# A GRU over 128 steps on one core: zero products during the loads, weight sums moved into the first step, x turned one step at a time, biases spread in two parts

## The chip, the cores and the metric

The kernel runs on one core of a Trainium2 chip. A core has TensorE (PE, with PEld for the loading of its stationary operand), VectorE (DVE), ScalarE (ACT), GpSimd (POOL) and SyncE (SP), which here only issues DMAs. The metric is the device time of one execution in microseconds; the median of several executions is compared.

## The reference

x is 64 sequences of 128 steps with 512 numbers each, `cond_1024` the first hidden state (64 x 512). The output is x plus the hidden states of a GRU:

```
for t in range(T):
    comb = concatenate([x_t, h])
    z = sigmoid(comb @ Wz + bz)
    r = sigmoid(comb @ Wr + br)
    h_cand = tanh(concatenate([x_t, r * h]) @ Wh + bh)
    h_new = (1 - z) * h + z * h_cand
    y_t = h_new
    h = tanh(h_new @ Wp + bp) if (t + 1) % 4 == 0 and t < T - 1 else h_new
return x + y
```

Wz, Wr and Wh are 1024 x 512: the upper 512 rows meet x (the kernel's `wx`), the lower 512 meet h or r*h (`wh`). Everything is float32.

## The kernel before

**Layout.** A state of 64 x 512 lies as 128 partitions x 256: partition s*64 + b holds half s of row b. A product with a 512 x 512 matrix is four units k in the order `ORDER`; each unit (`product`, through `products`, L177) is two matmuls, one for each half of the columns, written to the two halves of the partitions. A float32 matmul is two matmul records, so a unit is four records of 64 x 256. The stationary operand is the state turned round, 128 x 64. `turn` (L202) does the turning: eight bf16 transposes on PE into the two PSUM banks `turn_ps[0]` and `turn_ps[1]`, and one copy for each bank (L193) into `xT`, `hT` or `rhT`, on DVE or ACT as the caller says. The activations of a step use another part of the same two banks (`act_ps`).

**A step t** runs through these places in program order:

1. R: `product(slots[R], hT, wh[R], k)` for four k, onto a slot of PSUM that already holds the share of x and the bias
2. for t below 5, turns of x (`turn_x`, two of them), with their copies on ACT
3. `read_out`: pending read-outs of x products
4. sigmoid of R on ACT, `rh` = r*h on DVE (L599)
5. Z: four units; then the turn of rh, its copies on DVE; sigmoid of Z and of -Z on ACT, `keep` = (1-z)*h on DVE (L615)
6. `fill(places[0])`: units of x products for later steps, from `queue`
7. H: four units with `rhT`; `read_out`; tanh on ACT, two DVE operations for each half (L638, L643) that make h
8. `fill` again, the turn of h, between its halves a unit of `fill`; with every fourth step the extra product with `wp`
9. in steps 0 and 1, two more turns of x; then POOL's additions

Each engine takes its instructions in this program order; the schedule is by hand.

**Shares of x.** Step 0 gets its share directly (`first`), steps 1 to 7 by `plain(t)`, twelve units each, with a read-out of two DVE additions (L409, L414). In steps 0, 1 and 2 the queue holds `plain(2t+2)` and `plain(2t+3)`, and the places are 12, 9, 1 and 2 units. From step 8 on, four steps at a time are worked out together by `batches`, a two-level scheme of seven products in place of eight, which needs sums of blocks of `wx` and sums of the turned x:

- `sum_outer` (L300 to L302): six DVE subtractions and additions of 128 x 768 that fill `tw[2]`, `tw[3]`, `tw[4]` from `wx`; after it, `sum_inner` (L309 to L311) and for some blocks `sum_inner_1` (L314) on POOL: blocks 1, 2 and 3 from `wx`, blocks 6, 7 and 4 from `tw`.
- `sum_raw12`, `sum_s12` (L323 to L326, L341, L342), `sum_s34`: sums of turned x on POOL for one group of four steps. The first group of the batches is `FIRST` = 2, steps 8 to 11. x of steps 8 to 15 is read from two tiles `early`, whose buffers later hold batch results.
- The batches start in step 3, in the places of `fill`; step 3 also has three `sum_inner_1` on DVE before `rh`.

**The start.** SP issues x of steps 0 and 1 and half of each gate's `wx`, then `wh`, more of x, and `wp`; ACT issues the biases, the other halves of `wx` and the first state. The bias rows are spread over 64 partitions by matmuls with a row of ones (L160): four records of 512 columns into `rc` (R and H), four into `zp` (Z and p), then four DVE copies to `bias` and one POOL subtraction to `bias_d`. Then x of steps 0 and 1 is turned with copies on DVE, then come `first` and `plain(1)` unit by unit, with the turn of the first state after the R units. Before the step loop stand `read_out()`, `sum_outer()` on DVE and the eighteen plus three POOL operations of `sum_inner` and `sum_inner_1`.

Of the kernel before, what the change touches and what calls it, by code (L numbers as in the profile page):

```python
# [10 lines left out]
BF16 = mybir.dt.bfloat16  # L11
# [6 lines left out]
def kernel(  # L18
# [29 lines left out]
    nc = tc.nc  # L48
    B, T, D = x.shape
    H = h0.shape[1]  # L50
    P = 128
    S = 2
    N = H // S
# [4 lines left out]
    FIRST = 2  # L58
    R, Z, H_ = range(3)
# [4 lines left out]
    one = ctx.enter_context(tc.tile_pool(name="one", bufs=1))  # L64
# [74 lines left out]
    rc = ps_c.tile([P, 2, N], F32, name="rc")  # L139
    zp = ps_c.tile([P, 2, N], F32, name="zp")  # L140
    slots = (rc[:, 0, :], zp[:, 0, :], rc[:, 1, :])
    slot_p = zp[:, 1, :]
    scratch = [ps_c.tile([P, 2 * N], F32, name=f"scratch_{n}") for n in "qrax"]
# [9 lines left out]
    bias = const.tile([P, C, 4, P], F32, name="bias")  # L153

    def cut(ps):
        return ps.rearrange("p (c n) -> p c n", c=C)

    for a, ps in enumerate((rc, zp)):
        for s in range(S):
            nc.tensor.matmul(  # L160
                ps[s * B : (s + 1) * B, :, :],
                lhsT=ones,
                rhs=bias_row[:, 2 * a : 2 * a + 2, ts(s, N)],
                start=True,
                stop=True,
            )
    for i, ps in ((R, slots[R]), (H_, slots[H_]), (Z, slots[Z]), (3, slot_p)):
        nc.vector.tensor_copy(bias[:, :, i, :], cut(ps))
    bias0 = bias[:, 0, 0:3, :]
    bias_d = const.tile([P, 3, P], F32, name="bias_d")  # L170
    nc.gpsimd.tensor_sub(bias_d, bias[:, 1, 0:3, :], bias0)


    def products(ps, lhs, rhs, start=False):
# [11 lines left out]
    def product(ps, lT, w, k, start=False):  # L186
        s0, c0 = divmod(k, C)
        products(ps, lT[:, c0, ts(s0, B)], lambda s: w[:, k, ts(s, N)], start)
# [6 lines left out]
    def turn(src, dst, c, name, eng):  # L195


        pt = turn_ps[c][:, :P].bitcast(BF16).rearrange("p (w n) -> p w n", w=2)
        for s in range(S):
            words = src[:, c * P + s * B : c * P + (s + 1) * B].bitcast(BF16)  # L200
            for w in range(2):
                nc.tensor.transpose(  # L202
                    pt[s * B : (s + 1) * B, w, :],
                    words.rearrange("p (n w) -> p w n", w=2)[:, w, :],
                    ident16,
                )
        copy(
            eng,
            dst[:, c, :].bitcast(U16).rearrange("p (n w) -> p n w", w=2),
            pt.bitcast(U16).rearrange("p w n -> p n w"),  # L210
        )

    def new_T(tag, name):
        return two.tile([P, C, P], F32, tag=tag, name=name)
# [7 lines left out]
    def new_xT(g):  # L222
        if g not in xT:
            xT[g] = xtp.tile([P, Q4, C, P], F32, tag="xT", name=f"xT_{g}")

    def turn_x(t, eng=nc.scalar):
        g, i = divmod(t, Q4)
        new_xT(g)
        src = xr[g] if g < 2 else early[g]
        for c in range(C):  # L230
            turn(src[:, i, :], xT[g][:, i], c, f"xT_{t}", eng)
# [36 lines left out]
    def outer(kb, nb, ka):  # L268

        return wx[:, ka * C + kb, :, :].rearrange("p g (s n u) -> p n s g u", s=S, n=C)[:, nb]  # L270
# [12 lines left out]
    def inner(i, ka, na):  # L283
        return OPERAND[i](ka)[:, :, :, ts(na, P // 2)]
# [13 lines left out]
    def sum_outer():  # L298
        for ka in range(S):
            nc.vector.tensor_sub(tw[3][:, ka], outer(1, 1, ka), outer(0, 1, ka))  # L300
            nc.vector.tensor_add(tw[2][:, ka], tw[3][:, ka], outer(0, 0, ka))
            nc.vector.tensor_sub(tw[4][:, ka], outer(1, 0, ka), tw[2][:, ka])  # L302
# [5 lines left out]
    def sum_inner(i, eng):  # L308
        eng.tensor_sub(tt[:, i - 1, 1], inner(i, 1, 1), inner(i, 0, 1))  # L309
        eng.tensor_add(tt[:, i - 1, 0], tt[:, i - 1, 1], inner(i, 0, 0))  # L310
        eng.tensor_sub(tt[:, i - 1, 2], inner(i, 1, 0), tt[:, i - 1, 0])  # L311

    def sum_inner_1(i, eng):
        eng.tensor_sub(inner(i, 0, 1), inner(i, 0, 1), inner(i, 0, 0))  # L314
# [4 lines left out]
    def four(dst, top, low):  # L319

        half = B
        left, right = (lambda v: v[..., :half]), (lambda v: v[..., half:])
        nc.gpsimd.tensor_add(dst[0], left(low), right(low))  # L323
        nc.gpsimd.tensor_sub(dst[1], dst[0], left(top))
        nc.gpsimd.tensor_sub(dst[2], left(top), left(low))  # L325
        nc.gpsimd.tensor_sub(dst[3], right(top), dst[1])  # L326

    def sum_raw12(g):
        v = xT[g]
        sx[g, 12] = one.tile([P, 4, C, B], F32, tag="s12r", name=f"s12r_{g}")  # L330
        four([sx[g, 12][:, n] for n in range(4)], v[:, 0], v[:, 1])
# [6 lines left out]
    def sum_s12(g):  # L338
        v = xT[g]
        o = sx[g, "o12"] = one.tile([P, 2, 2, P], F32, tag="o12", name=f"o12_{g}")  # L340
        nc.gpsimd.tensor_add(o[:, 0], v[:, 2:4, 0, :], v[:, 2:4, 1, :])  # L341
        nc.gpsimd.tensor_sub(o[:, 1], o[:, 0], v[:, 0:2, 0, :])  # L342
        s = sx[g, 56] = one.tile([P, 4, 2, B], F32, tag="s56", name=f"s56_{g}")
        four([s[:, n] for n in range(4)], o[:, :, 0], o[:, :, 1])
# [45 lines left out]
    def fill(n):  # L390
        for _ in range(min(n, len(queue))):
            unit, end = queue.pop(0)
            unit()
            if end is not None:
                pending.append(end)

    def read_out():
        while pending:
            pending.pop(0)()
# [116 lines left out]
    def outer_u2(g):  # L516
        add(m_(g, 7), m_(g, 7), m_(g, 6))
# [11 lines left out]
    )  # L529


    turn_x(0, nc.vector)
    turn_x(1, nc.vector)
    h = h_init
    hT = new_T("hT", "hT_init")
    first = [
# [11 lines left out]
            for c in range(C):  # L548
                turn(h, hT, c, "hT_init", nc.vector)
    read_out()  # L550
    sum_outer()
    for i in (1, 2, 3, 6, 7, 4):
        sum_inner(i, nc.gpsimd)
        if i > 3:
            sum_inner_1(i, nc.gpsimd)

    for t in range(T):
        g, j = divmod(t, Q4)
# [2 lines left out]
        pair, u = divmod(t - 3, 8)  # L561
        even, odd = FIRST + 2 * pair, FIRST + 2 * pair + 1
# [12 lines left out]

        for k in ORDER:
            product(slots[R], hT, wh[R], k)
        if t == 0:
            turn_x(2)
            turn_x(3)  # L580
        elif t == 1:
            turn_x(6)
            turn_x(7)
        elif t == 2:
            turn_x(10)
            turn_x(11)
        elif t in (3, 4):
            turn_x(2 * t + 6)
            turn_x(2 * t + 7)
        read_out()  # L590
        if u == 0 and pair >= 1:
            outer_u2(odd - 2)
        if t == 3:
            for i in (1, 2, 3):
                sum_inner_1(i, nc.vector)
        rh = two.tile([P, N], F32, tag="rh", name=f"rh_{t}")
# [21 lines left out]
            nc.scalar.copy(cut(slot_p), bias[:, :, 3, :])  # L618
        if last:
            nc.gpsimd.tensor_add(xr[g][:, j, :], xr[g][:, j, :], keep)  # L620
        fill(places[0])


        for k in ORDER:
# [34 lines left out]
        if prop:  # L659
# [8 lines left out]
            for c in range(C):  # L668
                turn(h, hT, c, f"hpT_{t}", (nc.vector, nc.scalar)[c])
            fill(2)  # L670
        if t == 0:
            turn_x(4)
            turn_x(5)
        elif t == 1:
            turn_x(8)
            turn_x(9)


        if pair >= 0:
# [29 lines left out]
                    outer_c12(odd)  # L709
        if u == 7 and pair >= -1 and (even + 2) * Q4 < T:  # L710
            sum_raw12(even + 2)
            sum_s12(even + 2)
        if pair >= 0:
            if u in (1, 2):
                for n in range(2):
# [9 lines left out]
        n = 0  # L725
        if t >= T - CHUNK:
            n = {T - 2: 3, T - 1: 1}.get(t, 0)
        elif j == Q4 - 1:
            n = 4
# [58 lines left out]
```

## Time and profile before

| | us |
|---|---|
| median of 3 runs | 1371.43 (1371.06 to 1373.5) |
| the profiled execution | 1370.75 |
| its span, first to last instruction | 1368.9 |
| DVE busy | 689.2 (50%) |
| ACT busy | 631.2 (46%) |
| POOL busy | 938.7 (69%) |

The span is the time between the first and the last instruction of the profiled execution; the execution's own time also holds what lies around it. Busy times are sums over instructions; matmuls overlap, so that a record of 0.38 us can be followed by the next after 0.11. In a timeline line stand the start, the length, the engine, the line of the kernel, the operation, the tile written and the tiles read, the shape, and the number of instructions merged; in brackets the idle time before it and what ended it. "turn" is the pair of turn banks, `rc` and `zp` hold the slots of R and H, and of Z and p.

### The profile page before, as it was taken

How to read it: one execution, taken by the hardware profiler on the slowest of the kernel's cores; microseconds unless marked ns; L12 is line 12 of the kernel's file. 1: busy time of each engine (PE TensorE's matmuls, PEld its weight loads, DVE VectorE, ACT ScalarE, POOL GpSimd, SP SyncE). 2: the span in 40 equal slices, each digit the busy share in tenths (PEclk: the TensorE clock that was granted, in tenths of full speed). 3: DMA queues.
4: the chain of work that ended last, by engine and by line, in shares of the span. 5: the costliest groups of instructions: out<-in, count | busy, mean ns of one | idle time of the engine just before them, and what ended most of it. 6: DMA issues, size and time to landing. Idle time of an engine off the chain costs nothing.

```text
span 1368.9 us, 37448 instructions
## 1 busy us (share of the span) xinstructions
PE 1342.6 (98%) x15336; PEld 1028.9 (75%) x15336; DVE 689.2 (50%) x1875; ACT 631.2 (46%) x1857; POOL 938.7 (69%) x1139
## 2 busy tenths in 40 slices
PE   7999999999999999999999999999999999999996
PEld 4777777777777777777777777777777777777764
DVE  4245554555555555554555555555555555555543
ACT  1234445445444445445445444445445445454443
POOL 4327676787767786677686767786677686767740
PEclk9999999999999999999999999999999999999999
DMA  9002212212231222212222131222212222131010
GB/s 286 11 17 48 63 32 63 63 33 63 49 77 32 60 36 63 63 32 63 52 43 63 43 83 34 49 46 63 63 32 63 48 48 63 35 76 33 17 33 16
DMA packets 113572, 73.86 MB, mean 54 GB/s; under 512 B 61556, under 2 KB 109812, under 8 KB 113400
## 3 DMA queue, kind: packets, MB, share of 16 engines
q1 hardware_dynamic: 112336, 69.68, 22.5%
q8 instruction: 121, 1.98, 0.6%
q10 hardware_dynamic: 1064, 1.78, 0.4%
q14 instruction: 51, 0.42, 0.1%
HBM read 39.99 MB, written 16.78 MB: 41 GB/s over the span
## 4 chain that ended last, share of the span: by engine, by line
PE 96%; DMA 2%; DVE 1%; ACT 0%; issue 0%; SPq 0%; DVEq 0%; ACTq 0%
PE rc L177 33%; PE zp L177 20%; PE scratch_q L177 11%; PE scratch_x L177 10%; PE scratch_r L177 10%; PE turn L202 6%; PE scratch_a L177 6%; DMA early<-in_x_dram 1%; DMA wx<-in_L_cond_Wz_dram 1%; DMA wh<-in_L_cond_Wr_dram 1%; DVE h L643 0%; DVE turn L638 0%; ACT xT L193 0%; SPq L93 0%; DVE tw L300 0%
## 5 line engine op out<-in xcount | busy, mean ns | idle before, releaser
L177 PE MATMUL rc<-wh,rhT 128*64 128x256 f32 x2048 | 246.6, 381 | 2.0 <-ACT zp L614 2.0
L485 POOL TENSOR_TENSOR cp<-mb,mb 128x768 f32<-128x768 f32 x75 | 136.6, 1821 | 112.1 <-ACT rc L384 67.1
L177 PEld LDWEIGHTS rc<-wh,rhT 128*64 128x64 f32 x2048 | 158.9, 137 | 55.0 <-ACT zp L614 12.4
L177 PE MATMUL rc<-wh,hT 128*64 128x256 f32 x1536 | 183.1, 380 | 0.5 <-DVE hT L193 0.2
L177 PE MATMUL zp<-wh,hT 128*64 128x256 f32 x1536 | 183.2, 379 | 0.0
L722 POOL TENSOR_TENSOR xr<-xr,h 128x256 f32<-128x256 f32 x127 | 92.5, 729 | 102.1 <-DVE h L643 95.5
L193 DVE COPY rhT<-turn 128x256 uint16<-128x256 uint16 x256 | 96.8, 420 | 127.1 <-PE turn L202 127.1
L638 DVE TENSOR_TENSOR turn<-turn,z 128x128 f32<-128x128 f32 x256 | 75.5, 295 | 161.0 <-ACT turn L637 161.0
L485 POOL TENSOR_TENSOR cp<-mb 128x768 f32<-128x768 f32 x45 | 81.9, 1820 | 108.4 <-ACT rc L384 107.2
L177 PEld LDWEIGHTS zp<-wh,hT 128*64 128x64 f32 x1536 | 117.5, 137 | 47.4
L177 PEld LDWEIGHTS rc<-wh,hT 128*64 128x64 f32 x1536 | 111.6, 137 | 45.2 <-issue 1.0
L598 ACT ACTIVATE turn<-rc 128x128 f32<-128x128 f32 x256 | 55.4, 260 | 156.6 <-issue 85.6
L452 DVE TENSOR_TENSOR cx<-scratch_r,cx 128x384 f32<-128x384 f32 x105 | 58.6, 558 | 128.7 <-ACT cx L450 128.7
L193 ACT COPY hT<-turn 128x256 uint16<-128x256 uint16 x127 | 47.3, 373 | 155.8 <-PE turn L202 96.6
L485 POOL TENSOR_TENSOR mb<-mb,mb 128x768 f32<-128x768 f32 x60 | 109.2, 1820 | 13.4 <-DVE mb L460 13.4
L458 DVE TENSOR_TENSOR mb<-scratch_r,cq 128x384 f32<-128x384 f32 x105 | 58.6, 558 | 88.1 <-ACT cq L457 88.1
L384 ACT COPY rc<-cp 128x256 f32<-128x256 f32 x254 | 95.8, 377 | 11.6 <-POOL s L325 0.4
L637 ACT ACTIVATE turn<-rc 128x128 f32<-128x128 f32 x256 | 57.0, 262 | 90.3 <-PE rc L177 90.3
L613 ACT ACTIVATE z<-zp 128x256 f32<-128x256 f32 x128 | 49.2, 384 | 104.0 <-PE zp L177 104.0
L202 PEld LDWEIGHTS <-h 128*64 128x64 bf16 x1016 | 47.4, 109 | 51.0 <-DVE h L643 46.0
L384 ACT COPY zp<-cp 128x256 f32<-128x256 f32 x127 | 47.9, 377 | 78.1 <-DVE keep L615 78.1
L202 PE MATMUL turn<-ident,h 128*64 128x128 bf16 x1016 | 76.6, 227 | 5.4 <-DVE h L643 5.4
(149 smaller groups left out, 2954.6 us busy)
## 6 DMA issues: line engine op xcount, KB each, us to landing
xr<-in_x_dram SPq DMA_DIRECT2D x62, 256.0 KB, 4.2
out_dram<-xr SPq DMA_DIRECT2D x62, 256.0 KB, 3.3
xs<-in_x_dram SPq DMA_DIRECT2D x56, 256.0 KB, 4.3
wh<-in_L_cond_Wr_dram SPq DMA_DIRECT2D x2, 512.0 KB, 7.6
wh<-in_L_cond_Wz_dram SPq DMA_DIRECT2D x2, 512.0 KB, 8.3
wh<-in_L_cond_Wh_dram SPq DMA_DIRECT2D x2, 512.0 KB, 10.4
early<-in_x_dram SPq DMA_DIRECT2D x4, 256.0 KB, 13.1
wp<-in_L_cond_Wp_dram SPq DMA_DIRECT2D x1, 1024.0 KB
```

The source lines that it names most:

```text
L177: nc.tensor.matmul(ps[s * B : (s + 1) * B], lhsT=lhs, rhs=rhs(s), start=start, stop=True, skip_group_check=True,)
L193: (eng.copy if eng is nc.scalar else eng.tensor_copy)(dst, src)
L202: nc.tensor.transpose(pt[s * B : (s + 1) * B, w, :], words.rearrange("p (n w) -> p w n", w=2)[:, w, :], ident16,)
L384: nc.scalar.copy(cut(slots[i]), G[t][:, :, i, :])
L452: nc.vector.tensor_add(T2[n], r_ps, T2[n])
L458: nc.vector.tensor_add(blocks()[:, :, 0, 1], r_ps, q2)
L485: nc.gpsimd.tensor_add(dst, a, b)
L598: nc.scalar.activation(act_ps[c], slots[R][:, ts(c, P)], AF.Sigmoid)
L613: nc.scalar.activation(z, slots[Z], AF.Sigmoid)
L637: nc.scalar.activation(pc, slots[H_][:, ts(c, P)], AF.Tanh)
L638: nc.vector.tensor_mul(pc, pc, z[:, ts(c, P)])
L722: nc.gpsimd.tensor_add(xr[g][:, j, :], xr[g][:, j, :], h_new)
```

## The change

Four edits:

- A tile `zeros` (128 x 512 bf16) is cleared on POOL, and `idle(n)` issues n matmuls of zeros into `scratch[0]`: ten ahead of everything on PE, two before `first`.
- The spreading of the biases becomes `spread(a, ps)`: R and H before the turns of x, Z and p after them; each part's two copies to `bias` follow at once. The subtraction for `bias_d` comes after the second part.
- `sum_outer()` and POOL's sums of blocks 6, 7 and 4 move from before the loop into step 0, after `keep` and before `fill(places[0])`. POOL's sums of blocks 1, 2 and 3 stay before the loop.
- x is turned one step at a time, in three places: after R (x of steps 2, 5, 8, 11, 13, 15 in steps 0 to 5), before H (3, 6, 9 in steps 0 to 2) and at the end of the step (4, 7, 10, 12, 14 in steps 0 to 4). Before, two were turned in a place: after R (2 and 3, 6 and 7, 10 and 11, 12 and 13, 14 and 15 in steps 0 to 4) and at the end (4 and 5, 8 and 9 in steps 0 and 1). Since x of step 11 is now turned in step 3, `sum_s12(FIRST)` moves from the end of step 2 into step 3.

```diff
-    for a, ps in enumerate((rc, zp)):
+    def spread(a, ps):
         for s in range(S):
             nc.tensor.matmul(
                 ps[s * B : (s + 1) * B, :, :],
...
-    for i, ps in ((R, slots[R]), (H_, slots[H_]), (Z, slots[Z]), (3, slot_p)):
-        nc.vector.tensor_copy(bias[:, :, i, :], cut(ps))
+        for i in ((R, H_), (Z, 3))[a]:
+            nc.vector.tensor_copy(bias[:, :, i, :], cut((slots[i] if i < 3 else slot_p)))
+
     bias0 = bias[:, 0, 0:3, :]
     bias_d = const.tile([P, 3, P], F32, name="bias_d")
-    nc.gpsimd.tensor_sub(bias_d, bias[:, 1, 0:3, :], bias0)
+
+
+    zeros = one.tile([P, 2 * N], BF16, tag="cq", name="zeros")
+    nc.gpsimd.memset(zeros, 0.0)
+
+    def idle(n):
+        for _ in range(n):
+            nc.tensor.matmul(
+                scratch[0][:B, :], lhsT=zeros[:, :B], rhs=zeros, start=True, stop=True
+            )
...
+    idle(10)
+    spread(0, rc)
     turn_x(0, nc.vector)
     turn_x(1, nc.vector)
+    spread(1, zp)
+    nc.gpsimd.tensor_sub(bias_d, bias[:, 1, 0:3, :], bias0)
+    idle(2)
...
     read_out()
-    sum_outer()
-    for i in (1, 2, 3, 6, 7, 4):
+    for i in (1, 2, 3):
         sum_inner(i, nc.gpsimd)
-        if i > 3:
-            sum_inner_1(i, nc.gpsimd)
...
-        if t == 0:
-            turn_x(2)
-            turn_x(3)
-        elif t == 1:
-            turn_x(6)
-            turn_x(7)
-        elif t == 2:
-            turn_x(10)
-            turn_x(11)
-        elif t in (3, 4):
-            turn_x(2 * t + 6)
-            turn_x(2 * t + 7)
+        if t < 6:
+            turn_x((2, 5, 8, 11, 13, 15)[t])
...
         if t == 3:
+            sum_s12(FIRST)
             for i in (1, 2, 3):
                 sum_inner_1(i, nc.vector)
...
+        if t == 0:
+            sum_outer()
+            for i in (6, 7, 4):
+                sum_inner(i, nc.gpsimd)
+                sum_inner_1(i, nc.gpsimd)
         fill(places[0])
+        if t < 3:
+            turn_x((3, 6, 9)[t])
...
-        if t == 0:
-            turn_x(4)
-            turn_x(5)
-        elif t == 1:
-            turn_x(8)
-            turn_x(9)
+        if t < 5:
+            turn_x((4, 7, 10, 12, 14)[t])
...
-            sum_s12(even + 2)
+            if pair >= 0:
+                sum_s12(even + 2)
```

## The prediction

> **What bounds the kernel now.** I read the page first, then the chain of waits, then the timeline of the first 110 us engine by engine, since every line that the change touches runs there.
>
> ```profile
> PE 1342.6 (98%) x15336; PEld 1028.9 (75%) x15336; DVE 689.2 (50%) x1875; ACT 631.2 (46%) x1857; POOL 938.7 (69%) x1139
> PE 96%; DMA 2%; DVE 1%; ACT 0%; issue 0%; SPq 0%; DVEq 0%; ACTq 0%
> ```
>
> TensorE (PE) sets the end: it is idle 1368.9 - 1342.6 = 26.3 us in all. A microsecond taken off PE's stream, or out of a gap in it, comes off the end; work on the other engines counts only where PE waits for it. So I looked for where PE loses time early. There are three places. First the start, in PE's timeline:
>
> ```profile
> 7.03 0.64 PE L202 MATMUL turn<-ident,xr 128*64 128x128 bf16 x8
> ...
> 8.78 1.12 PE L177 MATMUL rc<-wx,xT 128*64 128x256 f32 x4
> 9.64 1.11 PE L177 MATMUL scratch_a<-wx,xT 128*64 128x256 f32 x4
> ...
> 13.05 0.63 PE L177 MATMUL scratch_a<-wx,xT 128*64 128x256 f32 x4
> 13.49 0.62 PE L177 MATMUL rc<-wx,xT 128*64 128x256 f32 x4
> ```
>
> Four matmul records follow each other 0.85 us apart until 13.05 and 0.43-0.44 us after: half clock, then full, though the clock column says 1.00 throughout. Second, step 0, in the timelines of VectorE (DVE) and of PE:
>
> ```profile
> 22.05 1.49 DVE L300 TENSOR_TENSOR tw<-wx 128x768 f32<-128x768 f32 x1
> ...
> 26.80 1.74 DVE L300 TENSOR_TENSOR tw<-wx 128x768 f32<-128x768 f32 x1
> 28.58 0.96 DVE L301 TENSOR_TENSOR tw<-tw,wx 128x768 f32<-128x768 f32 x1
> 29.57 0.96 DVE L302 TENSOR_TENSOR tw<-wx,tw 128x768 f32<-128x768 f32 x1
> 30.45 0.48 DVE L599 TENSOR_TENSOR rh<-turn,h_init 128x128 f32<-128x128 f32 x2
> ```
>
> ```profile
> 24.36 1.93 PE L177 MATMUL zp<-wh,hT_init 128*64 128x256 f32 x16
> 30.79 0.64 PE L202 MATMUL turn<-ident,rh 128*64 128x128 bf16 x8 [4.50 <-DVE rh L599]
> 31.22 4.77 PE L177 MATMUL scratch_q<-wx,xT 128*64 128x256 f32 x32
> ```
>
> rh stands in DVE's queue behind the six operations of sum_outer, and PE waits for rh. The windows by engine show the price in clock too (after the length of the window comes PE's busy time; the clock stands third from the end):
>
> ```profile
> 26.71:30.12 3.41, 0.00 (x0) 0.00 (x0) 3.34 (x4) 0.27 (x1) 1.52 (x2) 1.00 1.08 274
> 30.12:33.53 3.41, 2.74 (x20) 1.78 (x22) 1.90 (x6) 0.38 (x1) 3.25 (x4) 0.50 1.12 263
> ```
>
> One stretch of 3.41 us with no PE work is followed by 3.41 us at half clock. Third, the x transposes, which come in pairs, here between R and Z of step 1:
>
> ```profile
> 47.54 0.42 PE L202 MATMUL turn<-ident,xr 128*64 128x128 bf16 x8
> 47.89 1.41 ACT L193 COPY xT<-turn 128x256 uint16<-128x256 uint16 x4 [1.47 <-PE turn L202]
> 48.31 0.58 PE L202 MATMUL turn<-ident,xr 128*64 128x128 bf16 x8 [0.35 <-ACT xT L193]
> ...
> 48.70 1.93 PE L177 MATMUL zp<-wh,hT 128*64 128x256 f32 x16
> ```
>
> The second x of a pair needs the two turn banks that ScalarE (ACT) is still copying out. The pair holds PE from 47.54 to 48.70, 1.16 us.
>
> **The change part by part.** The sum is made against the profiled execution (1370.75 us, span 1368.9); the median of the runs shown, 1371.43, lies 0.7 above it.
>
> *sum_outer into step 0.* Z's last matmul issues at 24.36 + 16 x 0.108 = 26.08 and the turn of rh at 30.79: 4.71 us of gap. The turn then took 0.43 instead of 0.22 (50.43 to 50.65 in step 1), and the 32 + 16 matmuls of plain(2) and the start of H run from 31.22 to 37.54, 6.32 us instead of 48 x 0.108 = 5.18: 1.14 lost. Together 6.1 us. What is late next: rh without sum_outer. With one x turned before Z, ACT copies 0.7 us from R's end + 0.35, the two sigmoids follow, rh is done about 1.8 us after R's end (step 1's row with its copies halved); PE wants it after 0.22 + 1.73 = 1.95. It fits by 0.15-0.2 us. Where does the 6-operation block go? Behind keep on DVE, ahead of the read-out of plain(2) and of h. POOL's sums of blocks 1-3 start at 16.46 and take nine times about 1.03, to 25.7; keep ends near 25.6, so DVE is alone: 6 x 0.97 = 5.9 us, to about 31.7. H ends near 31.6, and the two read-outs (0.69 + 0.42) and h (1.3) end by 34.1, while PE has nine product units (9 x 0.43 = 3.9) and turns h at 35.5. Cover 1.4 us: cost 0. POOL's 12 sums of blocks 6, 7, 4 follow from 30.5 to 43, about as late as before (42.6), and are first used in step 3, beyond 75.
>
> [...] the rows beside POOL show 1.49-1.74, so 9.8 us by the row; alone 0.96. If the overlap stayed, h would end near 38 and PE lose 2.3 us by the row[...]. I take 0, because POOL's queue is empty at that time and its next sum needs sum_outer's fifth result.
>
> *x one at a time.* Seven pairs, start of the first turn to the next product: 1.15, 1.13, 1.16, 1.15, 1.16, 1.16, and in step 4 1.14 + 0.56 of waiting for rh (Z's end 103.23, turn 103.79): 8.6 us. After: 14 singles by 0.22 = 3.1. The places behind fill and at the step's end have free banks (last copied over 1 us before). Two stalls are new. In step 3 DVE runs without a break from 80.44 to rh at 85.46, and PE would now want rh 0.5 earlier; sum_s12 also moves to POOL beside it: 0.4 (0.2 to 1.2). In step 4 ACT's two copies of batch results stand before the sigmoid, and DVE's two sums before rh: 0.8 (0.5 to 1.1). Net gain 8.6 - 3.1 - 1.2 = 4.3. sum_s12 itself (about 3.4 us on POOL) is wanted by PE some 4 us after it ends; the x of steps 12-15, up to one step later, are still turned ahead of POOL's sums of them and of the batch results that refill their buffer.
>
> *The start.* No row shows a product of bf16 zeros; the nearest is the bias product (same 512 columns, 0.43 each at half clock): ten are 4.27 us. They can start once POOL has cleared zeros, about 1.8 (ones is done at 1.39), at the latest at 3.4, where PE's first record is. From 1.8: zeros to 6.1; with full clock from 6.2, biases R/H to 7.0; DVE copies biases, then xT_0, to 8.7 (four copies near 0.38); the turn of x_1 to 8.95, biases Z/p 0.86 to 9.8, two zeros 0.43, first product 10.25 instead of 8.78. Then 8 x 0.432 = 3.46, h 0.22, 2 x 3.46: R of step 0 starts at 20.85 instead of 21.48. Gain **0.6**. Loads don't stop it: no DMA is added or moved on SP's or ACT's queue, the last gate of wx is in by 16.46 (POOL's first sum waits for all), and is wanted at 17.4. If PE really starts at 3.4, -1.0.
>
> Does the clock open? [...] 30.12-33.53 was busy for 2.74 of 3.41 and opened it[...]. But 2.81-6.22, busy with bias products of one row for 2.79, did not open it, so the kind of product counts, and zeros are untried. Closed, the first product comes at 12.4 and R at 23.3 (open at 13.05) to 25.0 (16.46): 1.8 to 3.5 lost instead of 0.6 won. I take open, as zeros fill all 128 rows.
>
> Sum: 6.1 + 4.3 + 0.6 = 11.0; 1370.75 - 11.0 = 1359.75, and 1371.43 - 11.0 = **1360.4** as a median.
>
> **Rivals.** *The gate stays shut* through the zeros: 1360.4 + 2.4 to 4.1 = 1362.8 to 1364.5. For it: the window 2.81-6.22. Against: 128 rows. *DVE and POOL collide* in step 0 and step 3 (9.8 us of sum_outer): 2.3 + 0.8 more, 1363.5. *The stall does not go*, since rh or wh[Z] (landing not shown, used at 24.36, wanted at 22.8) is late anyway: only 4.9 of gain, 1366.5. *Slower:* each single x holds PE as a pair does, by the late sigmoid rather than by the banks, and one ACT copy (0.37) besides: 14 x 1.52 = 21.3 against 8.6 removed is 12.7 lost, 6.7 won elsewhere: 1377.4. It decides from (8.6 + 6.7)/14 = 1.1 us a place. Against it: the turn of rh takes 0.22, and the pair's wait is named, ACT xT.
>
> **Numbers.** Forecast 0.63 (its own range 1359 to 1362), gate shut 0.20, collision 0.11, stall stays 0.03, slower 0.03. The range 1358.4 to 1364.2 leaves out the last two and the edges. 0.2% is 2.7 us, about what a measurement here tells from nothing: faster 0.95, same 0.02, slower 0.03.
>
> **What would show it.** Matmul fours 0.43 apart from 10.3 on (0.85: gate shut); PE without a gap between Z of step 0 and rh's turn, and no half clock near 30; single turns of 0.22; waits for rh under 1 us in steps 3 and 4; sum_outer near 0.96 each. If singles hold PE longer than 1.1 us, or h of step 0 comes after 35.5, I am wrong.

## The result and the profile after

The changed kernel takes 1363.20 us (median of 6, 1362.49 to 1364.13), the kernel before 1371.24 beside it (6 runs, 1370.83 to 1373.5): a ratio of 0.9938, 95% interval 0.9926 to 0.9950. That is 8.0 us less. The profiled execution has a span of 1361.0 us, 7.9 less.

The page of the changed kernel, busy times and chain of waits:

```profile
PE 1341.8 (99%) x15348; PEld 1033.1 (76%) x15348; DVE 686.0 (50%) x1875; ACT 630.6 (46%) x1857; POOL 935.7 (69%) x1140
PE 98%; DVE 1%; ACT 0%; issue 0%; POOL 0%; DVEq 0%; POOLq 0%; ACTq 0%
```

PE is busy for nearly as long as before (1342.6), 4.5 us of it now with the ten zeros; its gaps shrank from 26.3 to 19.2 us. These totals do not show where. Cutting both timelines at the first R product of each step does:

| from R of step to R of step | before | after | gained |
|---|---|---|---|
| start to 0 | 21.48 | 23.15 | -1.67 |
| 0 to 1 | 24.33 | 16.66 | 7.67 |
| 1 to 2 | 18.31 | 16.68 | 1.63 |
| 2 to 3 | 17.15 | 16.67 | 0.48 |
| 3 to 4 | 17.36 | 16.69 | 0.67 |
| 4 to 5 | 10.20 | 9.84 | 0.36 |
| 5 to 6 | 9.67 | 11.21 | -1.54 |
| 6 to the end | 1250.4 | 1250.1 | 0.3 |

The sum is 7.9 us. All but 0.3 of it is made and lost in the first 111 us, and there are two losses: the start, and step 5.

**Step 0.** The timelines of DVE and of PE in the changed kernel:

```profile
26.11 0.49 DVE L602 TENSOR_TENSOR rh<-turn,h_init 128x128 f32<-128x128 f32 x2 [2.26 <-ACT turn L601]
...
27.89 0.41 DVE L618 TENSOR_TENSOR keep<-zp,h_init 128x256 f32<-128x256 f32 x1
28.22 0.95 DVE L310 TENSOR_TENSOR tw<-wx 128x768 f32<-128x768 f32 x1
...
33.05 0.96 DVE L312 TENSOR_TENSOR tw<-wx,tw 128x768 f32<-128x768 f32 x1
```

```profile
25.15 1.89 PE L187 MATMUL zp<-wh,hT_init 128*64 128x256 f32 x15
26.82 0.39 PE L212 MATMUL turn<-ident,rh 128*64 128x128 bf16 x7
27.05 0.38 PE L187 MATMUL scratch_q<-wx,xT 128*64 128x256 f32 x1
```

rh now comes before sum_outer, and no idle time is printed before its turn on PE. sum_outer takes 0.95 to 0.96 for each operation; POOL ran nothing from 25.8 to 33.1. (Before, the first four had POOL's sums beside them and took 1.49 to 1.74.) h was done at 36.0, and PE turned it at 38.07.

**The start.** The timeline of PE, and then the windows by engine, cut at the events of the clock:

```profile
1.90 4.47 PE L179 MATMUL scratch_q<-zeros 128*64 128x512 bf16 x10 [1.90 <-POOL zeros L175]
6.30 1.43 PE L160 MATMUL rc<-tt,ones 1*64 1x512 f32 x4
7.67 0.42 PE L212 MATMUL turn<-ident,xr 128*64 128x128 bf16 x8
8.93 0.64 PE L212 MATMUL turn<-ident,xr 128*64 128x128 bf16 x8 [0.84 <-DVE xT L203]
9.50 1.07 PE L160 MATMUL zp<-tt,ones 1*64 1x512 f32 x4
10.50 0.64 PE L179 MATMUL scratch_q<-zeros 128*64 128x512 bf16 x1
```

```profile
3.66:7.07 3.41, 3.41 (x9) 1.13 (x9) 0.00 (x0) 0.00 (x0) 0.00 (x0) 1.00 0.91 279
7.07:10.48 3.41, 2.55 (x24) 0.81 (x20) 2.17 (x6) 1.49 (x2) 0.00 (x0) 1.00 1.07 360
10.48:13.90 3.42, 3.42 (x18) 2.11 (x17) 0.76 (x2) 0.00 (x0) 1.00 (x1) 0.50 1.05 376
```

The clock changed at 7.07, 10.48 and 13.90, 3.41 us apart: a stretch of that length is called a window here, "open" is full clock (1.00 in the column) and "shut" half (0.50), and "gate" is a name for what switches. In the kernel before, the changes at 13.05 and 30.12 lie 17.07 us apart, five times 3.41; where a window is named that ends in no change of the column, it is counted off in steps of 3.41 from one that does, or from the point where products change their pace. The clock opened at 7.07, stayed open for the one window that held biases, transposes and waits (2.55 us of PE records in 3.41), and was shut again at 10.48, when the first product was about to run. It ran at half speed to 13.90. (Before 7.07 the column of this profile says 1.00 too, but the ten zeros are 0.43 apart, half speed: in the second profile with filled gaps, below, zeros at full clock are 0.22 apart.)

**Step 5.** The timelines of ACT, DVE and PE:

```profile
101.77 0.65 ACT L203 COPY xT<-turn 128x256 uint16<-128x256 uint16 x2 [1.47 <-PE turn L212]
102.30 0.50 ACT L467 COPY cq<-scratch_q 128x384 f32<-128x384 f32 x1
102.67 0.46 ACT L601 ACTIVATE turn<-rc 128x128 f32<-128x128 f32 x2
```

```profile
102.83 0.56 DVE L468 TENSOR_TENSOR mb<-scratch_r,cq 128x384 f32<-128x384 f32 x1 [3.75 <-ACT cq L467]
103.30 0.55 DVE L469 TENSOR_TENSOR mb<-scratch_x,cq 128x384 f32<-128x384 f32 x1
103.77 0.55 DVE L470 TENSOR_TENSOR mb<-scratch_q,cx 128x384 f32<-128x384 f32 x1
104.23 0.48 DVE L602 TENSOR_TENSOR rh<-turn,h 128x128 f32<-128x128 f32 x2
```

```profile
101.64 1.93 PE L187 MATMUL zp<-wh,hT 128*64 128x256 f32 x16
104.57 0.50 PE L212 MATMUL turn<-ident,rh 128*64 128x128 bf16 x8 [1.00 <-DVE rh L602]
```

The copies of x of step 15 wait on ACT for R's end. The copy of a batch result (L467) stands behind them, three DVE operations wait for it, and rh stands behind those three. Before, no turn was made in step 5, and the same copy ran just after R had begun (108.83), on ACT of the kernel before:

```profile
108.98 0.48 ACT L457 COPY cq<-scratch_q 128x384 f32<-128x384 f32 x1
110.82 0.43 ACT L598 ACTIVATE turn<-rc 128x128 f32<-128x128 f32 x2 [1.35 <-issue]
```

Step 4 has a smaller wait of this kind in the changed kernel:

```profile
94.24 0.50 PE L212 MATMUL turn<-ident,rh 128*64 128x128 bf16 x8 [0.54 <-DVE rh L602]
```

### The profile page after: what moved, and what is told of

It reads as the page before. It is cut to its first block, busy times and chain, and to the rows that moved or that the text cites. A ratio compares the mean times of both kernels' runs of the same rounds, so it can differ in the third digit from the quotient of the medians.

```text
span 1361.0 us, 37468 instructions
## 1 busy us (share of the span) xinstructions
PE 1341.8 (99%) x15348; PEld 1033.1 (76%) x15348; DVE 686.0 (50%) x1875; ACT 630.6 (46%) x1857; POOL 935.7 (69%) x1140
## 4 chain that ended last, share of the span: by engine, by line
PE 98%; DVE 1%; ACT 0%; issue 0%; POOL 0%; DVEq 0%; POOLq 0%; ACTq 0%
PE rc L187 33%; PE zp L187 20%; PE scratch_q L187 11%; PE scratch_x L187 11%; PE scratch_r L187 10%; PE scratch_a L187 6%; PE turn L212 6%; PE scratch_q L179 0%; DVE h L653 0%; DVE turn L648 0%; ACT z L616 0%; PE rc L160 0%; ACT turn L647 0%; ACT xT L203 0%; ACT zp L617 0%
```

## Experiments

Each is an edit of the changed kernel. "R of step 0" is the start of its first product, read from the one profiled execution. Each ratio is to the kernel before, measured again beside the experiment: its medians were 1371.77 to 1372.24, against 1371.24 beside the changed kernel. So a difference of under 1 us between medians of different experiments says little.

**Without the zeros.**

```diff
-    idle(10)
     spread(0, rc)
...
-    idle(2)
```

> The changed kernel without its twelve products of zeros; the spread in two parts and all else stay. Theory A (the zeros open the clock too early: the gate opens at 7.07, one-row bias products and transposes do not hold it, it shuts at 10.48 and the zeros only delay the first product): the first product comes near 9.1 instead of 10.5, half clock until about 13, R of step 0 near 21.9 instead of 23.15, and the time is about 1.2 us below the changed kernel's 1363.2. Theory B (the zeros do what they are for, and the one profile fell on a bad phase of the gate): R of step 0 later than 23.15, time 1 us or more above the changed kernel.

Measured: 1361.65 (1361.16 to 1362.12), ratio 0.9923 (0.9908 to 0.9937). The first product comes at 9.36, R of step 0 at 22.53. Theory A held in its direction: by the medians the kernel is 1.5 us faster without the zeros. R of step 0 came 0.6 later than it said, since the clock opened at 14.53 and not about 13.

**The start of the kernel before.**

```diff
-    idle(10)
     spread(0, rc)
+    spread(1, zp)
+    nc.gpsimd.tensor_sub(bias_d, bias[:, 1, 0:3, :], bias0)
     turn_x(0, nc.vector)
     turn_x(1, nc.vector)
-    spread(1, zp)
-    nc.gpsimd.tensor_sub(bias_d, bias[:, 1, 0:3, :], bias0)
-    idle(2)
```

> The changed kernel with the start of the kernel before: both bias parts spread first, no zeros; sum_outer in step 0 and single turns stay. Theory A: the start is worth -1.7, so R of step 0 falls back to 21.5 and the time is 1361.5. Theory B: the time is 1363.2 or more.

Measured: 1360.81 (1360.52 to 1361.58), ratio 0.9916 (0.9899 to 0.9932); first product at 8.88, R of step 0 at 21.63. By the medians the start's two edits together cost some 2.4 us. Spreading in two parts is no gain by itself: in the run above, without zeros, the first product came 0.5 later. The turn of x of step 0 had to wait until 5.80 for x itself to land (7.14 here), so it came 1.3 us earlier, and the second spread, which took 1.9 us from 7.46 on, now stood before the first product.

**sum_outer back before the loop.**

```diff
     read_out()
-    for i in (1, 2, 3):
+    sum_outer()
+    for i in (1, 2, 3, 6, 7, 4):
         sum_inner(i, nc.gpsimd)
+        if i > 3:
+            sum_inner_1(i, nc.gpsimd)
```

and the same lines taken out of step 0.

> The changed kernel with sum_outer and POOL's sums of blocks 6, 7, 4 back before the loop. My theory (rh stands behind sum_outer on DVE, and the gap shuts the clock for 3.4 us): PE idles about 4.5 us before the turn of rh in step 0, half clock follows, +5.7 us, 1368.9. Rival (the gap was kept by the pair of x turns or by late weights, not by sum_outer): under +2 us.

Measured: 1368.39 (1367.36 to 1369.86), ratio 0.9974 (0.9962 to 0.9986). Its PE timeline in step 0:

```profile
26.30 1.89 PE L187 MATMUL zp<-wh,hT_init 128*64 128x256 f32 x15
31.64 0.50 PE L212 MATMUL turn<-ident,rh 128*64 128x128 bf16 x8 [3.45 <-DVE rh L605]
31.97 3.63 PE L187 MATMUL scratch_q<-wx,xT 128*64 128x256 f32 x32
```

The wait for rh is back, so its cause is shown. In this profile R of step 0 to R of step 1 takes 20.45 us against 16.66: 3.8, not 5.7. Two things are smaller than I had put them. Five of the six operations ran in 0.95 to 0.96, with POOL nearly done with blocks 1 to 3 (one took 1.64). And the gap, shorter, did not shut the clock: the 32 product matmuls follow at full speed (31.97 to 35.43, 0.108 each). Each of the two windows that it touches (26.40 to 29.81 to 33.22) still held about 1.6 us or more of PE work, while the gap of the kernel before covered a whole one (26.71-30.12, 0.00 us). So the half clock in that profile, 1.4 of the 6.1 us, is not a fixed part of the stall's price: of these two gaps it followed the one that left a whole window empty. Of the 5.1 us between the spans another 1.1 is the start, with R of step 0 at 24.29.

**x in pairs again**, in the places of the kernel before; `sum_s12` of the first group stays in step 3.

```diff
-        if t < 6:
-            turn_x((2, 5, 8, 11, 13, 15)[t])
+        if t < 5:
+            turn_x((2, 6, 10, 12, 14)[t])
+            turn_x((3, 7, 11, 13, 15)[t])
...
-        if t < 3:
-            turn_x((3, 6, 9)[t])
...
-        if t < 5:
-            turn_x((4, 7, 10, 12, 14)[t])
+        if t < 2:
+            turn_x((4, 8)[t])
+            turn_x((5, 9)[t])
```

> The changed kernel with x turned in pairs as before (sum_s12 of the first group stays in step 3). My ledger of the two traces gives singles 4.8 us less of PE time in steps 0 to 4 and 1.5 us more in step 5, where the copies of x of step 15 stand before a batch read-out on ACT: net +3.2 us, 1366.4, and no wait for rh in step 5. Rival (the ledger mixes in other edits): within 1 us of 1363.2.

Measured: 1368.05 (8 runs, 1366.82 to 1369.98), ratio 0.9972 (0.9962 to 0.9982). From R of step 0 to R of step 6 it needs 91.57 us, the changed kernel 87.75: 3.8 us, 0.6 above the expected 3.2, of which 0.25 is a wait for rh in step 3 that neither other kernel has. No wait for rh in step 5. The profiled execution is the slowest of the eight, its span 7.2 us above that of the changed kernel: besides the 3.8 another 2.8 is the start, with R of step 0 at 25.93, and 0.6 lies after step 6. In this execution the ten zeros did not open the clock at all; fours of product matmuls stay 0.85 us apart to about 17.9.

**The read-out before the turn**, from step 4 on.

```diff
+        if t > 3:
+            read_out()
         if t < 6:
             turn_x((2, 5, 8, 11, 13, 15)[t])
         read_out()
```

> The changed kernel with one edit: in steps 4 and later the pending read-out is issued before the turn of x after R. My theory (in steps 4 and 5 the two copies of the turned x wait on ACT for R's end, and the batch read-out, the sigmoid and rh queue behind them): the waits for rh of 0.54 us in step 4 and 1.00 us in step 5 go, R of step 5 to R of step 6 falls from 11.2 to about 9.9 us, time about 1.9 us below the changed kernel. Rival (the turn of x itself before Z delays the sigmoid, whatever stands behind it): the waits stay within 0.3 us of what they were.

Measured: 1361.56 (4 runs, 1360.54 to 1363.57), ratio 0.9926 (0.9911 to 0.9940). No wait for rh is left in steps 4 and 5. R of step 4 to R of step 5 takes 9.09 us (9.84 in the changed kernel), R of step 5 to R of step 6 9.93 (11.21): 2.0 us, as my theory had it. The DVE timeline of step 5 there:

```profile
102.76 0.56 DVE L468 TENSOR_TENSOR mb<-scratch_r,cq 128x384 f32<-128x384 f32 x1 [1.63 <-ACT cq L467]
103.23 0.55 DVE L469 TENSOR_TENSOR mb<-scratch_x,cq 128x384 f32<-128x384 f32 x1
103.69 0.55 DVE L470 TENSOR_TENSOR mb<-scratch_q,cx 128x384 f32<-128x384 f32 x1
104.66 0.49 DVE L604 TENSOR_TENSOR rh<-turn,h 128x128 f32<-128x128 f32 x2 [0.42 <-ACT turn L603]
```

R of step 5 starts at 101.73 here: the three operations lie beside it, and rh waits for its sigmoid alone. The median shows 1.6 us of the 2.0. The start moves by itself by more than what is missing: in this profile, of the slowest of the four runs, R of step 0 lies at 25.94.

**Zeros in the gaps too.**

```diff
     turn_x(0, nc.vector)
+    idle(4)
     turn_x(1, nc.vector)
+    idle(2)
     spread(1, zp)
```

> The changed kernel with six more products of zeros between the turns of x 0 and 1 and the second spread. Theory A (the gate shut at 10.48 because only one-row products and transposes ran in its window): with the gaps filled the clock stays open once open, R of step 0 near 21.3 in executions where the ten zeros open it, and a time about 1.5 us below the changed kernel on average. Theory B (the gate counts something that zeros fill badly, or the phase decides alone): R of step 0 at 24 or later, time 1 us above the changed kernel or more.

Measured: 1366.31, 1360.41, 1366.20, 1366.18, 1360.65. In the profiled execution (1366.31) R of step 0 lies at 26.59 and the clock opens at about 17.6. The median says nothing here: the times fall into two groups.

**The same again, and the changed kernel again.**

> The kernel with six more zeros in the gaps once more, to see an execution in a good phase. Its times so far lie apart, 1360.4 and 1366.2. Theory A: where the ten zeros open the clock it stays open to the first product, R of step 0 near 21.3, time near 1360.4; in the other phases R of step 0 near 26.6, time near 1366. Times between 1362 and 1365 would speak against two kinds of start.

> The changed kernel once more, for the phase of the gate. Its ten zeros run from 1.9 to 6.3; a window of 3.41 us that is at least 2.7 us full of them opens the clock, and the window after it shuts it again. Theory A (start = phase): the granted clock shows either an opening between 5 and 7.3 followed by 3.4 us or more at half clock (R of step 0 at 23 to 24.5), or no opening before 16 (R of step 0 near 26). In no case R of step 0 before 22.5. Theory B: R of step 0 at 23.15 again whatever the windows are.

With filled gaps: 1361.54, 1363.18, 1360.87, 1360.42; the profiled one (1361.54) caught the other kind of start, in its windows by engine:

```profile
3.54:6.95 3.41, 3.41 (x9) 1.18 (x9) 0.00 (x0) 0.29 (x1) 0.00 (x0) 1.00 0.93 286
6.95:10.36 3.41, 3.39 (x30) 1.27 (x26) 2.17 (x6) 1.19 (x2) 0.00 (x0) 1.00 1.06 357
10.36:13.78 3.42, 3.42 (x32) 2.30 (x29) 0.76 (x2) 0.00 (x0) 1.00 (x1) 1.00 1.06 390
```

The gate opened within 0.12 us of where it did in the changed kernel's profile (6.95 and 7.07). With six zeros in the window that follows (6.95-10.36, 3.39 us of records against 2.55 in 7.07-10.48) it stayed open, and R of step 0 came at 21.82 instead of 23.15 (I had expected 21.3). So the shutting goes with the thin window: in all three profiles in which ten zeros opened the clock and the gaps were not filled (the changed kernel twice, sum_outer before the loop) it shut one window later, and in this one it did not. The time of 1363.18 is a miss: it fits neither kind, and no profile of such an execution was taken.

The changed kernel again: 1363.24 (1362.59 to 1364.00). Its windows by engine:

```profile
2.48:5.89 3.41, 3.41 (x10) 1.26 (x8) 0.00 (x0) 0.00 (x0) 0.00 (x0) 1.00 0.87 229
5.89:9.30 3.41, 2.55 (x24) 1.00 (x24) 1.98 (x6) 1.49 (x2) 0.00 (x0) 1.00 1.05 374
9.30:12.71 3.41, 3.41 (x15) 1.37 (x13) 0.95 (x3) 0.00 (x0) 1.00 (x1) 0.50 1.06 374
```

The clock opened at 5.89 (7.07 in the first profile), shut at 9.30 (10.48) and opened again at 16.13 (13.90); R of step 0 at 24.28 (23.15). Between these two profiles the phase, the place of the windows in the execution, moved the start, as theory A had it. The expectation's 2.7 us is what the window 3.66-7.07 of the first profile held of zeros; the window 2.48-5.89 here was full of them.

**What opens the clock.** Twenty zeros of one row in place of ten of 128, and two of one row before the first product.

```diff
-                scratch[0][:B, :], lhsT=zeros[:, :B], rhs=zeros, start=True, stop=True
+                scratch[0][:B, :], lhsT=zeros[:1, :B], rhs=zeros[:1, :], start=True, stop=True
...
-    idle(10)
+    idle(20)
```

> A measurement of the gate: in place of ten products of zeros over 128 rows, twenty over one row, and the two before the first product likewise over one row. Twenty take 8.5 us at half clock, so they hold at least one whole window of 3.41 us whatever its phase. If any matmul counts as activity, the gate opens before 10.4 and the twenty take less than 8.5 us. If only the rows in use count, as the bias products of the kernel before suggest, all twenty stay 0.43 us apart, and the clock opens only a whole window after the first product of x (near 17 or later).

Measured: 1369.12, a single execution. Its PE timeline:

```profile
1.90 8.31 PE L179 MATMUL scratch_q<-zeros 1*64 1x512 bf16 x19 [1.90 <-POOL zeros L175]
...
16.97 1.12 PE L187 MATMUL rc<-wx,xT 128*64 128x256 f32 x4
17.87 1.07 PE L187 MATMUL scratch_a<-wx,xT 128*64 128x256 f32 x4
...
20.43 0.83 PE L187 MATMUL rc<-wx,xT 128*64 128x256 f32 x4
21.09 0.60 PE L187 MATMUL scratch_a<-wx,xT 128*64 128x256 f32 x4
```

Twenty products, 8.5 us without a pause (1.90 to 10.43), did not open the clock; it opened about 4 us after the first product of x (16.97 to about 20.9). The bias spreads are products of one row too. Ten zeros over 128 rows, 4.4 us, opened it in four of the seven profiles that have them.

**Old start, read-out first.** The edits of "The start of the kernel before" and of "The read-out before the turn" together.

> Both findings together: the start of the kernel before (no zeros, biases in one piece before the turns), and the read-out before the turn of x from step 4 on; sum_outer in step 0 and single turns stay. Expected: 1361.5 less 1.9, about 1359.2 (1358.6 to 1359.8), below both kernels. If the parts interfere: 1360.5 or more.

Measured: 1359.48 (4 runs, 1358.40 to 1360.15), ratio 0.9908 (0.9893 to 0.9923), the lowest median of all, as expected. R of step 0 lies at 20.78 in its profile, in which the clock opened at about 11.5; from there to R of step 6 it takes 85.67 us, against 87.75 in the changed kernel.

| | R of step 0 | median |
|---|---|---|
| before | 21.48 | 1371.24 |
| changed (two profiles) | 23.15, 24.28 | 1363.20 |
| zeros, with other edits | 24.29, 25.93, 25.94 | |
| zeros in the gaps too (two profiles) | 26.59, 21.82 | |
| no zeros, spread in two parts | 22.53 | 1361.65 |
| old start | 21.63 | 1360.81 |
| old start, read-out first | 20.78 | 1359.48 |

## Why the prediction was right, and where it was not

The direction was right and the time lies in the range, but 2.8 us above the forecast. It also lies outside the forecast's own 1359 to 1362: the wider range holds it because it was drawn to take in the rivals, not because the start was understood. Of the three terms the first held, the second was 1.0 too high, and the third had the wrong sign. The forecast's sum was 6.1 + 4.3 + 0.6 = 11.0; the trace says 6.0 + 3.3 - 1.7 = 7.6, and 0.3 after step 6 that I do not assign.

- **sum_outer, 6.1.** R of step 0 to R of step 1 gained 7.67; 1.62 of that is two pairs of turns (1.15 + 1.13) less three singles (0.66), which leaves 6.0. Each sub-step held: rh in time, sum_outer alone on DVE, h done before its turn on PE (36.0 against 38.07, 2 us of cover where I had 1.4). The collision with POOL, the second rival, did not come, and neither did the third, that the stall stays.
- **x one at a time, 4.3.** In steps 0 to 4 the singles are worth 1.6 + 1.6 + 0.5 + 0.7 + 0.4 = 4.8. The stall of 0.8 in step 4 came as 0.7 (Z's end 93.53, turn of rh 94.24). The stall of 0.4 in step 3 did not come: the turn of rh follows Z directly at 76.84. The step that failed is "Two stalls are new. In step 3 [...] In step 4": I left step 5 out. I had looked for the batch's first read-out on ACT and not for its second, which in step 5 stood behind the added turn. It cost 1.5 us: 1.3 came back when the read-out was moved ahead, and 0.2 is the turn itself.
- **The start, 0.6.** The times of the units held: zeros from 1.90, first product at 10.51 where I had 10.25. The step that failed is "I take open": the clock opened, and I took it that it then stayed open. I had noted that one-row products had not opened it in 2.81-6.22, and did not ask what the same products and transposes would do to an open gate. Measured -1.7 instead of +0.6: from the first product to R of step 0 it took 12.64 us where I had 10.60, 2.0 of the 2.3 that were missed, and hardly less than the 12.70 before.
- **The rival "the gate stays shut"** gave 1362.8 to 1364.5, which holds the measured time, but by another way: here the gate opened and shut again. It stayed shut through the zeros in the profiles of the pairs and of the moved read-out (R of step 0 near 25.9) and in the first with filled gaps (26.59), later than the 23.3 to 25.0 of this rival.
- **"Does the clock open?"** A window with 2.7 us of zeros in 3.41 opened it (3.66-7.07, zeros to 6.37), as 2.74 us had in 30.12-33.53 of the kernel before; windows with 2.1 and 2.4 us of zeros did not (0.58-3.99 and 3.99-7.40 in the first profile with filled gaps). The burst of 4.4 us opened it in four of the seven profiles with ten zeros of 128 rows, too few to tell the shares.

## What to carry to other kernels

Before filling idle time of PE with products to raise its clock, add up what runs between the filling and the work that is to profit. Here a window of one-row products, transposes and waits (2.55 us of records in 3.41) undid it, and the filling with the split spread had pushed the first useful product from 8.8 to 10.5; no profile with zeros started step 0 before those with the old start (20.78 to 21.63). And when an instruction is added to an in-order queue, go through everything that any step issues behind it until the next wait that matters: each turn of x needs 0.22 us of PE, and one of them cost another 1.3 through ACT and DVE.

## What had not been expected of the hardware

- Twenty bf16 products of one row, 8.5 us back to back, left the clock at half in the one profile that has them; ten products of zeros over 128 rows, 4.4 us, opened it in four profiles of seven. So zeros as data did not keep it shut in those four.
- The clock shut while PE looked busy: 2.55 of 3.41 us of records in the window 7.07-10.48, all biases and transposes. With six zeros of 512 columns, 0.22 us each, in such a window (6.95-10.36 with filled gaps, 3.39 us of records) it stayed open. Whether transposes help to open it is not settled: in the kernel before, 2.31 us of products and 0.43 of transposes opened the clock in 30.12-33.53, while 2.48 us of products and zeros after one-row products did not in 11.12-14.53 of the run with pairs.
- The phase of the windows differed between executions: the clock first opened at 7.07 and at 5.89 in the two profiles of the changed kernel, and at 6.95 and about 17.6 in the two with filled gaps. The latter started step 0 at 21.82 and at 26.59, and the nine times of that kernel run from 1360.41 to 1366.31.
